# Differential attention in small blocks: the order of a software pipeline, and the place of a gelu

## The chip, the cores and the metric

The kernel runs on one core of a Trainium2 chip. A core has a matrix engine (TensorE, PE in the profile), a vector engine (VectorE, DVE), a scalar engine for activation functions (ScalarE, ACT), a general engine (GpSimd, POOL) and a queue engine (SyncE, SP). Each engine works through its own list of instructions in order and meets the others at semaphores. The metric is the device time of one execution in microseconds; lower is better.

## The reference, cut to what matters

The network is a chain of attention and feed-forward blocks on `x` of 2 x 1024 x 256, all in float32. The change is in the block that computes a differential attention with causal mask (16 heads of width 16 with two score matrices each, 4 key heads), in whose course the feed-forward block that follows it is computed too:

```python
q = _rope((x @ Wq).reshape(b, s, H, 2 * D))
k = _rope((x @ Wk).reshape(b, s, KVH, 2 * D))
v = (x @ Wv).reshape(b, s, KVH, D)
...
energy = jnp.einsum('bqhad,bkhad->bahqk', qd, kd)
energy = jnp.where(causal, NEG, energy)
scores = jax.nn.softmax(energy / np.sqrt(D), axis=-1)
diff = scores[:, 0] - lam * scores[:, 1]
diff = jnp.where(causal, NEG, diff)
diff = jax.nn.softmax(diff, axis=-1)
att = jnp.einsum('bhqv,bvhd->bqhd', diff, v)
att = att * jax.lax.rsqrt(jnp.mean(att * att, axis=-1, keepdims=True) + EPS) * rms_w
att = att * (1.0 - LAM_INIT)
return att.reshape(b, s, E) @ Wo
...
gelu = jnp.tanh(0.7978845608028654 * (gate + 0.044715 * gate ** 3)) * gate * 0.5 + gate * 0.5
out = jnp.einsum('tn,hn->th', gelu * up, Wd)
```

Here `b` is 2 and the sequence has 1024 tokens. There are two softmaxes in a row: one over the scores of each of the two matrices, and one over their difference.

## The kernel before

The stage is `attn_d_ffn1`. It goes over eight tiles `i` of 128 tokens, each for both batches. A tile has 16 pairs (two batches, eight pairs of heads each), so there are 128 pairs, and the loop at the end of the function runs one round `n` for each pair, with some more to drain. Tile `i` has `(i + 1) * 128` keys. The 64 pairs of tiles 0 to 3 (up to 512 keys) are *small*, the others *large*: these take their scores in two parts (`scores(0)`, `scores(1)`), and other PSUM pools are allocated at round 64.

A pair is an object with the steps of the work on two heads `h`, each with two score matrices `a`:

- `scores` (L1051, PE): four matmuls into two PSUM tiles `e`, of which there are two buffers, so that the next pair's scores need the maxima of this one.
- `highest` (L1062, DVE): four instructions that add the mask, write the negated scores to `p` and leave the negated row maxima in `nm`.
- `exponentials` (L1073, ACT): four activations in place, each with the row sum in `sm`.
- `ratio` (L1081, L1082 on DVE; L1086, L1090 on POOL): the reciprocals and quotients of the sums, then for each head a scaling of the second matrix and a select that masks its diagonal block.
- `difference` (L1099 on DVE; L1102, L1103 on POOL): for each head the difference of the two matrices with its row maximum, then the sign and the subtraction of the maximum.
- `turn(h)` (L1110 on PE, L1114 on ACT): the transposes of one head into the PSUM tile `dT`, of which there is one buffer, and the exponential on the way out into `pT`.
- `weigh` (L1127, PE): the product with the values, for two pairs at a time; L1136 on DVE turns the result once for eight pairs.

Every pair passes through the steps in later and later rounds: in round `n` there run the scores, maxima and exponentials of pair `n`, ratio and difference of pair `n-1`, the turns of pair `n-2` and `weigh` for pair `n-3`. The order in which they are called is the order on each engine: in this stage PE, DVE, ACT and POOL run in the order of the program (`in_order`).

Between these steps lie the *fill* steps of a round, from the table `at`: the layer norm, queries and keys of the next tile (`attn_d_inputs`, `attn_d_block`: matmuls L232, rope L259 and L268 on DVE, sums L273 and L976 on POOL, transposes L1001 and L1007, the copies L992 and L1002 on ACT), the output of the tile before (`attn_d_out`), and the feed-forward block of the tile before (`ffn1_parts`): `gate` and `up` matmuls in eight steps each (L1260; the gate's copy L1266 on ACT, the product with up L1268 on DVE), one `gelu` over the whole hidden layer (L1271, ACT) and the `down` matmuls (L1277). With `n` the first round of the tile after, gate runs in rounds `n+8` to `n+11`, gelu in `n+11`, up in `n+13` to `n+16` and down in `n+17` to `n+20`. A round's list is cut in three: a third before the first turn, a third between the turns, the rest at the end.

Of the kernel before, what the change touches and what calls it, by code (L numbers as in the profile page):

```python
# [13 lines left out]
AF = mybir.ActivationFunctionType  # L14
# [30 lines left out]
class Net:  # L45
# [772 lines left out]
    def attn_d_ffn1(self, w, wo, cos, sin, nlam, rms_w, deq):  # L818

        nc, tc = self.nc, self.tc
        NH, NKV, D = 16, 4, 16
        with ExitStack() as ctx:
            big = ctx.enter_context(tc.tile_pool(name="d_big", bufs=1))
            work = ctx.enter_context(tc.tile_pool(name="d_work", bufs=2))
            ps = ctx.enter_context(tc.tile_pool(name="d_ps", bufs=1, space=PSUM))
            self.ps = tc.alloc_tile_pool(name="d_ps0", bufs=1, space=PSUM)  # L830
            self.small = True

            nc.vector.tensor_scalar(
                wo, wo, rms_w, 1.0 - (0.8 - 0.6 * math.exp(0.0)), ALU.mult, ALU.mult
            )

            in_g = big.tile([P, 4], F32, name="in_g")
            nc.gpsimd.memset(in_g, 1.0)
            for pattern, base, cm in (([[-32, 4]], 0, 1), ([[32, 4]], 15, -1)):
                nc.gpsimd.affine_select(  # L840
                    out=in_g, in_=in_g, compare_op=ALU.is_ge, fill=0.0, base=base,
                    pattern=pattern, channel_multiplier=cm,
                )
            half = big.tile([P, 2], F32, name="half")
            nc.vector.tensor_reduce(half[:, 0:1], in_g, AX.X, ALU.add)
            nc.vector.tensor_scalar(half[:, 1:2], half[:, 0:1], -1.0, 1.0, ALU.mult, ALU.add)

            mask = big.tile([P, T], BF16, name="mask")
            nc.gpsimd.memset(mask[:, 0 : T - P], 0.0)
            nc.gpsimd.tensor_copy(mask[:, T - P : T], self.neg)  # L850
            ctx.enter_context(self.in_order())

            kT = [big.tile([P, 2, T], F32, name=f"kT{b}") for b in range(B)]
            v = [big.tile([P, NB, NKV, 32], F32, name=f"v{b}") for b in range(B)]
            for b in range(B):
                nc.gpsimd.memset(v[b][:, :, :, D:32], 1.0)
            pools = (ps, work, w, cos, sin, half, nlam, mask)
            at, pairs = {}, []  # L860

            def add(n, *steps):
                at.setdefault(max(n, -1), []).extend(steps)

            for i in range(NB):
                n = 16 * i
                tile_ = type("tile", (), {})()
                blocks = [
                    self.attn_d_block(pools, tile_, b, i, kT[b], v[b]) for b in range(B)
                ]  # L870
                for m, step in zip(
                    (-9, -8, -6, -4, -4, -2, -2, -2, -1, -1, -1, -1, -1),
                    (*self.attn_d_inputs(ps, work, tile_, i), *blocks[0][0], *blocks[1][0]),
                ):
                    add(n + m if i else -1, step)
                for _, units in blocks:
                    pairs.extend(units)

                n += 16
                squares, root, normalize, project = self.attn_d_out(ps, work, tile_, wo, i)  # L880
                if i == NB - 1:

                    for m, step in enumerate((squares, root, normalize, project)):
                        add(n + 2 + m, step)
                    continue
                stats, rows, turn, gate, gelu, up, down = self.ffn1_parts(ps, work, i, deq)
                for m, step in (
                    (2, squares), (3, root), (4, normalize), (5, project), (5, stats), (6, rows),
                    (7, turn), *((8 + k // 2, gate[k]) for k in range(8)), (11, gelu),
                    *((13 + k // 2, up[k]) for k in range(8)),  # L890
                    *((17 + k // 2, down[k]) for k in range(8)),
                ):
                    add(n + m, step)
            nothing = type("nothing", (), {"large": False})()

            def pair(n):
                return pairs[n] if 0 <= n < len(pairs) else nothing

            def do(u, name, *args):
                f = getattr(u, name, None)  # L900
                if f:
                    f(*args)

            for step in at[-1]:
                step()
            for n in range(max(at) + 1):
                if n == 16 * 4:

                    self.ps.release()
                    self.ps = tc.alloc_tile_pool(name="d_ps1", bufs=1, space=PSUM)  # L910
                    self.small = False
                fill = at.get(n, [])
                k = (len(fill) + 2) // 3, (2 * len(fill) + 2) // 3
                u, last, turned, weighed = (pair(n - j) for j in range(4))
                do(u, "scores", 0)
                do(u, "highest", 0)
                if not u.large:
                    do(u, "exponentials")
                do(weighed, "weigh")
                do(last, "ratio")  # L920
                for step in fill[: k[0]]:
                    step()
                do(turned, "turn", 0)
                if u.large:
                    u.scores(1)
                    u.highest(1)
                for step in fill[k[0] : k[1]]:
                    step()
                do(turned, "turn", 1)
                if u.large:  # L930
                    u.exponentials()
                do(last, "difference")
                for step in fill[k[1] :]:
                    step()
            self.ps.release()
# [22 lines left out]
    def attn_d_block(self, pools, tile_, b, qb, kT, v):  # L958

        nc = self.nc  # L960
# [50 lines left out]
        def pair(t, s):  # L1011

            own = type("pair", (), {})()
# [53 lines left out]
                if j == 1:  # L1067
                    nc.vector.tensor_tensor(own.nm, own.nm, nm, ALU.min)

            def exponentials():  # L1070
                for h in range(2):
                    for a in range(2):
                        nc.scalar.activation(  # L1073
                            own.p[h][a], own.p[h][a], AF.Exp,
                            bias=own.nm[:, h, a : a + 1], scale=-1.0,
                            accum_out=own.sm[:, h, a : a + 1],
                        )

            def ratio():

# [36 lines left out]
            for f in (scores, highest, exponentials, ratio, difference, turn):  # L1117
                setattr(own, f.__name__, f)
# [118 lines left out]
    def ffn1_parts(self, ps, work, i, deq):  # L1237


        nc = self.nc  # L1240
        wg, wu, wd = deq
        f = type("ffn", (), {})()
# [26 lines left out]

        def gelu():  # L1270
            nc.scalar.activation(f.inter, f.inter, AF.Gelu_apprx_tanh)  # L1271

        def down(b, quarter):
            if b == quarter == 0:
                f.po = self.bank(ps, "po").rearrange("p (b c) -> p b c", b=B)
            for m in range(4 * quarter, 4 * quarter + 4):
                nc.tensor.matmul(  # L1277
                    f.po[:, b], f.inter[:, m, b * P : (b + 1) * P],
                    wd[:, m % 2, (m // 2) * C : (m // 2 + 1) * C],
                    start=(m == 0), stop=(m == 15),  # L1280
                )
            if quarter == 3:
                xs = self.x[:, b * NB + i, :]
                nc.vector.tensor_tensor(xs, xs, f.po[:, b], ALU.add)

        return (
            stats, rows, turn, [lambda m=m: hidden(m, wg) for m in range(8)], gelu,
            [lambda m=m: hidden(m, wu) for m in range(8)],
            [lambda b=b, q=q: down(b, q) for b in range(B) for q in range(4)],
# [643 lines left out]
```

## Time and profile before

| what | value |
| --- | --- |
| time, median of 3 runs | 3122.29 us (3122.12 to 3124.22) |
| the profiled execution: time | 3129.27 us |
| its span, from first to last instruction | 3127.5 us |
| PE busy | 2628.4 us, 84% |
| DVE busy | 1923.2 us, 61% |
| ACT busy | 1351.5 us, 43% |
| POOL busy | 1031.1 us, 33% |
| mean granted clock of PE | 0.896 |

The stage of the change begins at about 1157 us (first scores, L1051) and its last scores are at 2261 us. Its groups are among the costliest of the page; each row gives line, engine, operation, output and input, count, busy time, mean duration in ns, then the idle time of the engine just before and what ended it:

```profile
L1062 DVE CUSTOM_DVE_ANT_0 p<-e,mask 128x512 f32<-128x512 f32 (+3 forms) x768 | 381.7, 553 | 106.2 <-PE e L1051 104.9
L1073 ACT ACTIVATE p<-p,nm 128x128 f32<-128x128 f32 (+7 forms) x512 | 389.9, 764 | 97.8 <-DVE nm L1062 88.2
L1086 POOL TENSOR_SCALAR p<-p,ra,neg_lam 128x128 f32<-128x128 f32 (+7 forms) x256 | 223.0, 871 | 235.3 <-DVE ra L1082 180.9
L1099 DVE CUSTOM_DVE_ANT_0 p<-p,rs 128x128 f32<-128x128 f32 (+7 forms) x256 | 207.8, 833 | 70.0 <-POOL p L1090 69.8
L1114 ACT ACTIVATE pT<-dT 128x128 f32<-128x128 f32 (+7 forms) x256 | 165.6, 647 | 285.8 <-PE dT L1110 284.5
```

The means mix blocks of 128 to 1024 keys. The column on idle time is read as: DVE stood idle for 70.0 us before the differences, nearly all of it until POOL's select at L1090 had ended.

### The profile page before, as it was taken

Reading aid. Unit: us, or ns where it says so; the run is one execution under the profiler, and the core shown is the slowest. Engines: PE = TensorE matmul, PEld = TensorE weight load, DVE = VectorE, ACT = ScalarE, POOL = GpSimd, SP = SyncE. Lnnn points to the kernel's source line nnn. Section 1 sums busy time; section 2 is a strip of 40 time slices with the busy share of each in tenths; the row PEclk is TensorE's granted clock in tenths of the full one; section 3 lists DMA queues with packets and bytes.
Section 4 is the critical chain, followed back from the end, with each engine's and each line's share of the span. In section 5 each row is a group of like instructions: output and inputs, shape, how many; then the busy total and the mean of one; then the engine's idle time right before and its main releaser. Section 6 shows DMA issues by size and latency. Waiting matters only on the chain.

```text
span 3127.5 us, 66883 instructions
## 1 busy us (share of the span) xinstructions
PE 2628.4 (84%) x26384; PEld 1618.6 (52%) x26384; DVE 1923.2 (61%) x6646; ACT 1351.5 (43%) x2712; POOL 1031.1 (33%) x1648
## 2 busy tenths in 40 slices
PE   6888889699998866887888888878878798988898
PEld 2233245343433433555555555555556577767777
DVE  4776650466765446676676777768835665665552
ACT  2785942144454335555655564655722121221110
POOL 3454210211202446565665565556620000000000
PEclk9999999699998975888899889888988899999999
DMA  3000000000000100000000000000010111001000
GB/s 112 1 1 1 1 1 0 0 1 1 1 1 26 42 15 1 1 1 1 1 1 1 1 1 1 1 1 1 1 32 16 23 23 23 14 18 36 22 10 14
DMA packets 61978, 35.38 MB, mean 11 GB/s; under 512 B 43216, under 2 KB 58080, under 8 KB 61664
## 3 DMA queue, kind: packets, MB, share of 16 engines
q1 hardware_dynamic: 59472, 29.49, 3.6%
q8 instruction: 208, 3.41, 0.4%
q10 hardware_dynamic: 2192, 1.61, 0.2%
q14 instruction: 106, 0.87, 0.1%
HBM read 22.68 MB, written 8.39 MB: 10 GB/s over the span
## 4 chain that ended last, share of the span: by engine, by line
PE 36%; DVE 13%; ACT 7%; issue 4%; POOL 3%; DMA 0%; POOLq 0%; ACTq 0%; DVEq 0%
PE ph L1260 5%; PE po L1767 4%; PE pg L1754 4%; DVE p L1062 4%; PE pu L1754 4%; PE e L1051 4%; ACT p L1073 4%; PE dT L1110 3%; POOL p L1086 2%; DVE p L1099 2%; PE po L1277 2%; PE py L1127 1%; PE pq L1437 1%; PE kh L1437 1%; PE pa L1437 1%
## 5 line engine op out<-in xcount | busy, mean ns | idle before, releaser
L1062 DVE CUSTOM_DVE_ANT_0 p<-e,mask 128x512 f32<-128x512 f32 (+3 forms) x768 | 381.7, 553 | 106.2 <-PE e L1051 104.9
L1073 ACT ACTIVATE p<-p,nm 128x128 f32<-128x128 f32 (+7 forms) x512 | 389.9, 764 | 97.8 <-DVE nm L1062 88.2
L1086 POOL TENSOR_SCALAR p<-p,ra,neg_lam 128x128 f32<-128x128 f32 (+7 forms) x256 | 223.0, 871 | 235.3 <-DVE ra L1082 180.9
L1110 PE MATMUL dT<-ident,p 128*128 128x128 f32 x1152 | 200.4, 307 | 113.0 <-ACT pT L1114 29.8
L1114 ACT ACTIVATE pT<-dT 128x128 f32<-128x128 f32 (+7 forms) x256 | 165.6, 647 | 285.8 <-PE dT L1110 284.5
L1051 PE MATMUL e<-kT,qT 32*128 32x512 f32 (+3 forms) x1536 | 234.2, 626 | 28.0 <-DVE nm L1062 26.7
L1099 DVE CUSTOM_DVE_ANT_0 p<-p,rs 128x128 f32<-128x128 f32 (+7 forms) x256 | 207.8, 833 | 70.0 <-POOL p L1090 69.8
L196 POOL TENSOR_SCALAR ln_mv<-ln_mv 128x2 f32<-128x2 f32 x48 | 15.7, 327 | 710.9 <-DVE ln_mv L194 701.0
L1110 PEld LDWEIGHTS dT<-ident,p 128*128 128x128 f32 x1152 | 154.5, 158 | 173.4 <-POOL p L1090 49.5
L723 ACT ACTIVATE pr<-s 128x512 f32<-128x512 f32 (+3 forms) x384 | 157.1, 496 | 170.2 <-PE s L718 167.0
L1103 POOL TENSOR_SCALAR p<-p,md 128x128 f32<-128x128 f32 (+7 forms) x256 | 208.3, 814 | 25.4
L437 ACT ACTIVATE pr<-s 128x1024 f32<-128x1024 f32 (+1 forms) x192 | 146.2, 823 | 122.0 <-PE s L431 119.4
L1754 PE MATMUL pg<-xT,gate 128*128 128x256 f32 x576 | 154.6, 415 | 11.0 <-issue 5.5
L1767 PE MATMUL po<-down,inter 128*128 128x256 f32 x576 | 156.8, 434 | 3.2 <-issue 2.0
L683 PE MATMUL s<-kT,qT 32*128 32x512 f32 (+3 forms) x768 | 152.4, 539 | 2.3 <-ACT pr L723 1.3
L442 ACT ACTIVATE pr<-pr 128x1024 f32<-128x1024 f32 (+1 forms) x192 | 153.1, 863 | 0.0
L691 DVE CUSTOM_DVE_ANT_0 masked<-s,mask 128x128 f32<-128x128 f32 (+3 forms) x256 | 110.7, 487 | 56.1 <-PE s L683 55.7
L1754 PE MATMUL pu<-xT,up 128*128 128x256 f32 x576 | 142.2, 391 | 0.0
L445 POOL TENSOR_SCALAR_AFFINE_SELECT pr<-pr 128x256 f32<-128x256 f32 x128 | 93.4, 746 | 143.2 <-ACT pr L442 81.9
L456 PE MATMUL py<-pr,v 128*32 128x512 f32 (+3 forms) x768 | 114.2, 531 | 27.0 <-POOL pr L445 24.9
L1767 PEld LDWEIGHTS po<-down,inter 128*128 128x128 f32 x576 | 123.5, 219 | 25.8 <-issue 2.8
L1760 DVE TENSOR_TENSOR inter<-inter,pu 128x512 f32<-128x512 f32 x72 | 49.3, 685 | 142.1 <-PE pu L1754 142.1
(302 smaller groups left out, 5446.2 us busy)
## 6 DMA issues: line engine op xcount, KB each, us to landing
uk_d<-uk SPq DMA_DIRECT2D x128, 32.0 KB, 1.9
r<-uk_d SPq DMA_DIRECT2D x8, 512.0 KB, 3.3
x<-in_L_attn_a_X SPq DMA_DIRECT2D x4, 512.0 KB, 6.1
qh_d<-qh SPq DMA_DIRECT2D x8, 256.0 KB, 2.7
o<-qh_d SPq DMA_DIRECT2D x128, 16.0 KB, 1.7
out<-x SPq DMA_DIRECT2D x4, 512.0 KB, 3.1
w<-in_L_ffn_W2T SPq DMA_DIRECT2D x1, 1024.0 KB, 8.0
pk<-in_L_ffn_gate_packed SPq DMA_DIRECT2D x8, 128.0 KB, 2.4
```

What stands on the lines that cost most here:

```text
L723: nc.scalar.activation(pr[:, g, off:512], tiles[g][:, 0:m], AF.Exp, scale=0.25)
L1051: nc.tensor.matmul(own.tiles[h][:, a, 0 : hi - lo], made["q"][r : r + 32, a, t, :], kT[r : r + 32, a, lo:hi], start=True, stop=True,)
L1062: nc.vector.tensor_tensor_reduce(own.p[h][a][:, lo:hi], own.tiles[h][:, a, 0 : hi - lo], neg_row[:, T - nk + lo : T - nk + hi], -1.0, 3e38 ...
L1073: nc.scalar.activation(own.p[h][a], own.p[h][a], AF.Exp, bias=own.nm[:, h, a : a + 1], scale=-1.0, accum_out=own.sm[:, h, a : a + 1],)
L1086: nc.gpsimd.tensor_scalar(p1, p1, own.ra[:, h : h + 1], nlam[:, head : head + 1], ALU.mult, ALU.mult)
L1099: nc.vector.tensor_tensor_reduce(p0, p0, p1, own.rs[:, h, 0:1], -3e38, ALU.add, ALU.max, md)
L1103: nc.gpsimd.tensor_scalar(p0, p0, md, 1.0, ALU.add, ALU.mult)
L1110: nc.tensor.transpose(dT[:, kb, :], own.p[h][0][:, kb * P : (kb + 1) * P], self.ident)
L1114: nc.scalar.activation(pT[:, 0 : qb + 1, :], dT[:, 0 : qb + 1, :], AF.Exp)
L1260: nc.tensor.matmul(ph[:, j, :], w[:, kc, m * P : (m + 1) * P], f.xT[:, kc, :], start=(kc == 0), stop=(kc == 1),)
L1754: nc.tensor.matmul(ph[:, j, :], m_[:, kc, m * P : (m + 1) * P], f.xT[:, kc, :], start=(kc == 0), stop=(kc == 1),)
L1767: nc.tensor.matmul(f.po[:, b], inter[m // 2][:, m % 2, b * P : (b + 1) * P], wd[:, m % 2, (m // 2) * C : (m // 2 + 1) * C], start=(m == 0) ...
```

## The change

For pairs 0 to 62 the difference moves from one to two rounds after the scores, the turns from two to three, `weigh` from three to four; the ratio stays at one. Pair 63, the last small one, keeps the old distances for difference and turns, so that it shares rounds 64 and 65 with pair 62. The large pairs keep theirs.

In a small round the order of calls is now: scores, weigh, first turn, gelu (if one is due), maxima, exponentials of the first head, two thirds of the fill, second turn, ratio, exponentials of the second head, difference, the rest of the fill. `exponentials` takes the head as its argument for this.

The gelu carries a mark `long`; such a step is taken out of the fill and run after the first turn, in the large rounds too. It is due in round `n+12` in place of `n+11`, and for tiles 0 to 2 the whole feed-forward block and the output steps come one round later than before, so that there the gelu comes in the 13th round.

```diff
                 stats, rows, turn, gate, gelu, up, down = self.ffn1_parts(ps, work, i, deq)
+                n += 1 if i < 3 else 0
...
-                    (7, turn), *((8 + k // 2, gate[k]) for k in range(8)), (11, gelu),
+                    (7, turn), *((8 + k // 2, gate[k]) for k in range(8)), (12, gelu),
...
+            first_large = 16 * 4
+            ratios, differences, turns, weighings = {}, {}, {}, {}
+            for m, u in enumerate(pairs):
+                a, b = (2, 3) if m < first_large - 1 else (1, 2)
+                for steps, lag in (
+                    (ratios, 1), (differences, a), (turns, b), (weighings, b + 1)
+                ):
+                    steps.setdefault(m + lag, []).append(u)
...
-                fill = at.get(n, [])
+                fill = [step for step in at.get(n, []) if not hasattr(step, "long")]
+                long = [step for step in at.get(n, []) if hasattr(step, "long")]
                 k = (len(fill) + 2) // 3, (2 * len(fill) + 2) // 3
-                u, last, turned, weighed = (pair(n - j) for j in range(4))
-                do(u, "scores", 0)
-                do(u, "highest", 0)
-                if not u.large:
-                    do(u, "exponentials")
-                do(weighed, "weigh")
-                do(last, "ratio")
+                u = pairs[n] if n < len(pairs) else nothing
+                if n < first_large:
+                    u.scores(0)
+                    do(weighings, n, "weigh")
+                    do(turns, n, "turn", 0)
+                    for step in long:
+                        step()
+                    u.highest(0)
+                    u.exponentials(0)
+                    for step in fill[: k[1]]:
+                        step()
+                    do(turns, n, "turn", 1)
+                    do(ratios, n, "ratio")
+                    u.exponentials(1)
+                    do(differences, n, "difference")
+                    for step in fill[k[1] :]:
+                        step()
+                    continue
+                if u.large:
+                    u.scores(0)
+                    u.highest(0)
+                do(weighings, n, "weigh")
+                do(ratios, n, "ratio")
                 for step in fill[: k[0]]:
                     step()
-                do(turned, "turn", 0)
+                do(turns, n, "turn", 0)
+                for step in long:
+                    step()
                 if u.large:
                     u.scores(1)
                     u.highest(1)
...
         def gelu():
             nc.scalar.activation(f.inter, f.inter, AF.Gelu_apprx_tanh)
+
+        gelu.long = True
```

More of the change, by code (lines that the diff above doesn't have):

```diff
@@ L894, in attn_d_ffn1, with do @@
             nothing = type("nothing", (), {"large": False})()
[L896 to L902, printed above, removed]
+            first_large = 16 * 4
[6 more added lines that the diff above has]
+                    steps.setdefault(m + lag, []).append(u)
+            def do(steps, n, name, *args):
+                for u in steps.get(n, []):
+                    f = getattr(u, name, None)
+                    if f:
+                        f(*args)
             for step in at[-1]:
                 step()
-            for n in range(max(at) + 1):
-                if n == 16 * 4:
+            for n in range(max(max(at), max(weighings)) + 1):
+                if n == first_large:
                     self.ps.release()
@@ L928, in attn_d_ffn1 @@
                     step()
-                do(turned, "turn", 1)
+                do(turns, n, "turn", 1)
                 if u.large:
-                    u.exponentials()
-                do(last, "difference")
+                    u.exponentials(0)
+                    u.exponentials(1)
+                do(differences, n, "difference")
                 for step in fill[k[1] :]:
@@ L1068, in highest, with exponentials @@
                     nc.vector.tensor_tensor(own.nm, own.nm, nm, ALU.min)
[L1070 to L1077, printed above, removed]
+            def exponentials(h):
+                for a in range(2):
+                    nc.scalar.activation(
+                        own.p[h][a], own.p[h][a], AF.Exp,
+                        bias=own.nm[:, h, a : a + 1], scale=-1.0,
+                        accum_out=own.sm[:, h, a : a + 1],
+                    )
             def ratio():
```

## The prediction

> **What bounds the kernel now.** I read the page's engine totals (no engine above PE's 84%), then the busy time by stretch, then the chain of waits and the waits inside one tile. The change lies in the differential attention stage, from about 1157 to 2290 us; its small half (blocks of up to 512 keys, rounds 0 to 63) lasts from 1160.0 to 1582.4. I cut it at the starts of the ratio (L1081): tile 0, then tiles 1, 2, 3 in two parts each, about seven rounds without and nine with gate and up matmuls. Columns: stretch, length, then busy us (instructions) of PE, weight load, DVE, ACT, POOL, granted clock, DMA share, GB/s.
>
> ```profile
> 1160.00:1230.70 70.70, 42.41 (x255) 22.97 (x254) 39.14 (x257) 37.30 (x169) 48.39 (x139) 0.58 0.00 1
> 1230.70:1269.20 38.50, 25.69 (x150) 12.92 (x151) 28.50 (x136) 19.45 (x73) 26.11 (x61) 0.50 0.00 1
> 1269.20:1332.70 63.50, 56.02 (x352) 41.67 (x351) 37.43 (x163) 38.88 (x111) 34.93 (x82) 0.94 0.01 1
> 1332.70:1380.70 48.00, 37.70 (x254) 24.21 (x253) 34.90 (x138) 24.00 (x72) 31.03 (x61) 0.79 0.00 1
> 1380.70:1449.10 68.40, 59.51 (x403) 42.94 (x402) 44.49 (x163) 44.44 (x109) 40.74 (x82) 0.95 0.00 1
> 1449.10:1506.30 57.20, 43.46 (x296) 26.77 (x295) 40.43 (x138) 28.54 (x72) 36.10 (x61) 0.76 0.00 1
> 1506.30:1582.40 76.10, 65.01 (x461) 45.98 (x459) 51.77 (x170) 47.81 (x105) 46.98 (x82) 0.96 0.01 1
> ```
>
> First parts: every engine idles a quarter or more of the time, so a loop of waits sets them. Second parts: PE is busy 85 to 88%. The chain shows the loop, here one turn of it in tile 3 from the last of four equal maxima:
>
> ```profile
> 1462.09 0.60 DVE p L1062
> 1462.83 0.17 DVE ra L1082
> 1463.17 0.77 POOL p L1086
> 1464.01 0.29 POOL p L1090
> 1464.31 1.28 POOL p L1086
> 1465.65 0.30 POOL p L1090
> 1465.98 0.75 DVE p L1099
> ```
>
> DVE takes the maxima of pair n, then the ratio of n-1, then stands until POOL has scaled n-1 (2.8 us), then takes the difference of n-1, and only then the next maxima. A second loop has the same length: ACT exponentiates n (L1073), then copies the turned block of n-2 out of PSUM (L1114, an exponential too; "copy" below), PE needs that copy for its second turn, and the next scores stand behind that turn. The waits of rounds 49 to 55 show both:
>
> ```profile
> ACT p L1073 <- DVE nm L1062: 18.6, 7, 4.8
> ...
> PE dT L1110 <- ACT pT L1114: 7.9, 4, 2.8
> ```
>
> The gelu is bracketed by two table loads; ACT is held for 6.2 us, and the next turn on PE comes 5.27 us late:
>
> ```profile
> 1289.69 1.28 ACT L1271 ACT_TABLE_LOAD   x1
> ...
> 1290.99 3.62 ACT L1271 ACTIVATE inter<-inter 128x4096 f32<-128x4096 f32 x1
> ...
> 1294.62 1.28 ACT L1073 ACT_TABLE_LOAD   x1
> ...
> 1298.40 0.66 PE L1110 MATMUL dT<-ident,p 128*128 128x128 f32 x2 [5.27 <-ACT v L992]
> ```
>
> **What the Trainium skill says.** "ScalarE: Activation LUTs", What ACT_TABLE_LOAD costs: each switch to another set of functions is a load of about 1283 ns plus a drain. The trace agrees on 1283 ns. "SBUF — State Buffer", Who interferes with whom: a DVE instruction with two SBUF inputs and a GpSimd instruction that reads SBUF exclude one another. The trace agrees: POOL's second scaling takes 1.28 us where the difference starts beside it, the first 0.77. So POOL cannot overlap the differences freely, and I price it by its means, lock included. "TensorE: Matmul & The Clock Gate", What's actually happening: an idle PE falls to half clock until it has been busy for a while. The trace has clock 0.50 to 0.79 in the first parts, 0.94 to 0.96 in the second; four transposes take 1.08 us after a gap, 0.60 otherwise.
>
> **The change, part by part.** The same instructions are issued; their order differs only in the small half and around the seven gelus.
>
> *One round more.* Difference n-2 now finds its input a round old, so DVE no longer waits for POOL. The new limit of a round without filling is the larger of two figures from mean durations. POOL, for two heads (scale + select + md + shift), tile 3: 2 x (0.90 + 0.31 + 0.25 + 0.79) = 4.5, 4.7 in the rounds measured. The loop turn, copies and exponentials, ratio, scaling, first shift, which now spans two rounds: 0.60 + 4.2 + 0.35 + 2.4 + 1.0 + 0.5 for hops (my estimate, from gaps of 0.05 to 0.2 between rows) = 9.1, or 4.6 a round. So 4.7 against 6.4 to 6.5 now. The same sum gives 2.9 against 3.5 for tile 0 (POOL 2.65, loop 5.7/2), 3.4 against 4.8 for tile 1, 4.0 against 5.4 for tile 2.
>
> Tile 0: about ten plain rounds at 0.6 = 6, and about 4 from its three long rounds (7.7, 4.4 and 10.6 us with the queries and keys), where DVE no longer meets ratio and difference in one chain: 10.
> First parts of tiles 1 to 3: the busiest engine plus a tenth for in-order losses gives 31.5 of 38.5, 40 of 48.0 and 46 of 57.2 (there PE's 43.5 is stretched by clock 0.76, so I lean on DVE's 40.4): 7 + 8 + 11 = 26.
>
> *Exponentials split around the second turn; scores, weigh and first turn ahead of the maxima.* PE gets its turned block free before ACT exponentiates, which takes away the second loop. In the second parts PE then sets the time. Its idle there is 7.5 + 8.9 + 11.1 = 27.5 us. I take 12: some 5 us a tile stays with PE waiting for queries and keys (matmul, rope on DVE, sum on POOL, transposes), and some with the gelu. The new wait: second exponentials stand on ACT behind the second copy, hence behind PE's fill. They end 0.6 + 1.6 = 2.2 us after that turn; DVE asks for them after the next scores and maxima, 1.1 + 2.5 = 3.6 us after it. Margin 1.4 us, so I price it at nothing. Queued behind that ratio on DVE are the difference and the next maxima.
>
> *Gelu.* In the small half it goes to round 13, which has no other fill, between first copy and first exponentials: still 6.2 us of ACT, with about 2 us of slack before the ratio, and PE's next first turn now waits for it. Inside the 12 above. In the large half (four gelus) it moves from the end of round 11 to behind the first copy of round 12. Near 2036 us ACT went exponentials, load, gelu, load, copy, PE's turn of 1.74, copy, exponentials: 10.0 us between the exponentials. New: first copy 0.7 wait + 0.92, 6.2, v copy 0.2, second copy 0.92 = 8.9 with the turn hidden under the gelu. 1.1 here, 0.5 near 1689, and PE's up matmuls start some us earlier; I take 1.3 x 4 = 5. From both sides: 0 and 4 x 3 = 12.
>
> *Feed-forward one round later* for tiles 0 to 2: no DMA moves, no queue of SP is passed; nothing. Hidden under 64 following rounds. *The hand-over at round 64* packs two differences and two turns into rounds 64 and 65: DVE 1.5, PE 1.2, ACT 1.2 us more there; -2.
>
> Sum: 10 + 26 + 12 + 5 - 2 = 51. In-order queues rarely reach such sums: I keep four fifths, 42. The profiled execution is 3129.27 (span 3127.5), hence 3087; the median of the runs shown lies 7 below it, so 3080 there.
>
> **Rivals.**
> A, my forecast: 3080 (gain 30 to 55).
> B, POOL and the lock become the wall: differences run beside POOL's work in every round and POOL's ops stretch to their largest (1.28, 1.34) for one more op per head: +1.1 us in the some 30 plain rounds, 33 of the 42 gone: 3113. For it: POOL is at 4.7 of the new round. Against: the differences overlap POOL's work already now.
> C, everything overlaps, PE's clock rises too: first parts at the busiest engine with PE at full clock, most of the 27.5 idle recovered, about 65: 3057. Against: queries and keys keep their serial chain.
> D, slower: the new wait of second exponentials behind PE's fill. Price: 27 rounds with gate and up; if the ratio is late by 2.0 us in each, 54 are lost and 12 of net loss remain: 3134. It decides from 42/27 = 1.6 us a round, 3.0 beyond where I put the end of the exponentials. For it: turn 1 now has two thirds of the fill ahead. Against: the margin of 1.4 and a full round of slack before the difference.
>
> **Numbers.** A 0.64, B 0.17, C 0.10, D 0.06, and 0.03 for a change that does nothing because another loop has the same length. The range runs from C's edge, 3057, to 3105, within B, to leave a fifth outside. About 0.2% is what a measurement of this kernel can tell from no change. Faster 0.91, within 0.03, slower 0.06.
>
> **What would show it.** Right: DVE's wait for POOL's select (L1090) all but gone in the small half, ratio to ratio 4.6 to 5.0 us in tile 3's plain rounds, clock in the first parts above 0.8, small half near 382 us instead of 422, large half shorter by 2 to 8. Wrong: ACT's second exponentials ending the wait of the ratio (D), POOL near 95% with its means up (B), or the second parts unchanged.

## The result and the profile after

The changed kernel takes 3168.22 us (median of 4 runs, 3156.69 to 3174.66), the kernel before 3122.36. The ratio is 1.0141, with a 95% interval of 1.0111 to 1.0172: slower by 1.4%, where the prediction had 1.3% faster. The profiled execution has a span of 3169.2 us against 3127.5, so 41.7 us more.

All of it lies in the small half: from the first maxima of pair 64 to the end it is 1555.1 us in both profiles. The first view is again the busy time by stretch, cut at the ratios of the same pairs as before (now L1111; pairs 16, 23, 32, 39, 48, 55 and 64): tile 0, then tiles 1 to 3 in two parts each. Nearly all the gate and up matmuls lie in the second parts, in both kernels. Columns: stretch, length, busy us (instructions) of PE, weight load, DVE, ACT, POOL, granted clock, DMA share, GB/s.

```profile
1160.00:1225.30 65.30, 39.28 (x252) 21.70 (x250) 37.45 (x251) 34.17 (x163) 46.65 (x134) 0.61 0.00 1
1225.30:1264.80 39.50, 23.94 (x133) 12.22 (x134) 29.14 (x144) 18.33 (x71) 25.93 (x63) 0.50 0.00 0
1264.80:1344.90 80.10, 60.46 (x369) 44.02 (x367) 36.52 (x152) 40.22 (x116) 35.14 (x82) 0.82 0.00 1
1344.90:1396.90 52.00, 35.66 (x232) 24.85 (x225) 35.84 (x145) 21.56 (x66) 30.16 (x61) 0.83 0.00 1
1396.90:1480.60 83.70, 62.31 (x424) 44.52 (x426) 44.03 (x153) 45.91 (x115) 41.28 (x82) 0.88 0.00 1
1480.60:1539.70 59.10, 40.77 (x271) 28.06 (x264) 42.79 (x146) 26.32 (x67) 34.81 (x61) 0.83 0.00 1
1539.70:1625.80 86.10, 66.76 (x476) 46.96 (x476) 51.94 (x164) 49.44 (x109) 49.64 (x86) 0.90 0.00 1
```

Lengths against before: tile 0 5.4 us shorter; the first parts 1.0, 4.0 and 1.9 longer; the second parts 16.6, 15.3 and 10.0 longer. Together 43.4, about as much as the whole. Nearly all of it is in the second parts, whose rounds have the most fill. PE's busy time over all seven stretches is the same (329.2 us, 329.8 before): what was added is waiting.

Who waits for whom, in the small half of the kernel before and then of the kernel after. A row gives engine, operand and line of the waiter, the releaser, us in total, times, longest:

```profile
DVE p L1099 <- POOL p L1090: 64.5, 74, 1.6
...
PE dT L1110 <- POOL p L1090: 26.2, 17, 2.6
...
PE dT L1110 <- ACT pT L1114: 22.6, 17, 2.8
...
PE dT L1110 <- ACT v L992: 16.0, 3, 5.4
...
PE dT L1110 <- POOL p L1103: 11.3, 9, 3.5
```

```profile
PEld dT L1140 <- POOL p L1133: 134.6, 72, 4.6
PE dT L1140 <- POOL p L1133: 92.0, 49, 4.2
...
PE dT L1140 <- ACT pT L1144: 27.6, 23, 5.8
...
DVE p L1129 <- POOL p L1120: 0.5, 3, 0.2
```

The change does remove the wait that it went for: the difference waited 64.5 us for POOL's select before, now 0.5. Its place is taken by another. PE's transposes (and the weight loads in front of them, which stand idle at the same time, so the two rows aren't added) wait for POOL's *shift*, the last of POOL's four operations on a head (L1103 before, L1133 now): 92.0 us on the matmul, 11.3 before.

The other three rows of PE before need care. The profile puts a wait for several semaphores down to the one that changed last. In all 37 waits of these rows the turn began 0.14 us after the end of an ACT copy out of `dT`, as in the row that names it, and in the rows of the shift 0.05 us after the end of a shift. So all three rows are waits for ACT's copy, 64.8 us, and the kernel after has 28.6 (27.6, and 1.0 in two more waits of this kind). The turns' waiting thus fell by 36 us for the copy and rose by 81 for the shift; the net 44 us are about what the small half grew by.

The chain of waits shows how that comes, in round 14 of tile 2. Columns: start, duration, engine with operand and line; the short "issue" pieces and some links are left out:

```profile
1442.37 0.87 PE dT L1140 x3
1443.24 5.74 PE ph L1290 x16
...
1449.01 0.69 DVE inter L1298
...
1449.82 0.17 DVE ra L1112
...
1450.16 1.26 POOL p L1116
...
1451.49 0.29 POOL p L1120
1451.79 0.65 POOL p L1116
...
1453.07 0.59 POOL p L1133
...
1453.71 0.55 PE dT L1140 x3
```

From one first turn to the next it is 11.3 us, and every link is in one round. PE turns a block and then does the fill (16 up matmuls, slow here: a gelu has just held PE up, and the granted clock in this piece is 0.61; the 16 of the next round take 3.46 us at 1.00). DVE's product with up waits for them. DVE's ratio stands behind that product, in the order of the program. POOL's scaling of pair n-1 needs the ratio, and POOL's shift of pair n-2 stands behind the scaling. PE begins the next round with the turn of exactly that pair. So the difference got a round of slack from POOL's scaling, but the turn did not get one from the shift, and the fill of PE now lies inside the loop.

### The profile page after: what moved, and what is told of

Its sections match the earlier page's. It is cut to its first block, busy times and chain, and to the rows that moved or that the text cites. A ratio compares the mean times of both kernels' runs of the same rounds, so it can differ in the third digit from the quotient of the medians.

```text
span 3169.2 us, 66946 instructions
## 1 busy us (share of the span) xinstructions
PE 2625.6 (83%) x26384; PEld 1623.9 (51%) x26384; DVE 1927.4 (61%) x6646; ACT 1346.7 (42%) x2712; POOL 1029.0 (32%) x1648
## 4 chain that ended last, share of the span: by engine, by line
PE 37%; DVE 12%; ACT 6%; POOL 5%; issue 5%; DMA 0%; POOLq 0%; ACTq 0%; DVEq 0%
PE ph L1290 5%; PE po L1799 5%; PE pg L1786 4%; PE pu L1786 4%; ACT p L1103 3%; PE dT L1140 3%; DVE p L1093 3%; PE e L1082 3%; PE po L1309 3%; POOL p L1116 2%; DVE p L1129 1%; PE py L1157 1%; PE pq L232 1%; PE pq L1469 1%; PE kh L1469 1%
## 5 line engine op out<-in xcount | busy, mean ns | idle before, releaser
L1103 ACT ACTIVATE p<-p,nm 128x128 f32<-128x128 f32 (+7 forms) x512 | 389.7, 765 | 12.4 <-DVE nm L1099 11.2
L1116 POOL TENSOR_SCALAR p<-p,ra,neg_lam 128x128 f32<-128x128 f32 (+7 forms) x256 | 229.7, 897 | 239.3 <-DVE ra L1112 156.3
L1133 POOL TENSOR_SCALAR p<-p,md 128x128 f32<-128x128 f32 (+7 forms) x256 | 205.0, 801 | 25.3
L1290 PE MATMUL ph<-xT,up 128*128 128x256 f32 x448 | 124.9, 432 | 28.0 <-DVE inter L1298 21.0
```

The costliest lines, as they stand in the source:

```text
L1103: nc.scalar.activation(own.p[h][a], own.p[h][a], AF.Exp, bias=own.nm[:, h, a : a + 1], scale=-1.0, accum_out=own.sm[:, h, a : a + 1],)
L1116: nc.gpsimd.tensor_scalar(p1, p1, own.ra[:, h : h + 1], nlam[:, head : head + 1], ALU.mult, ALU.mult)
L1133: nc.gpsimd.tensor_scalar(p0, p0, md, 1.0, ALU.add, ALU.mult)
L1290: nc.tensor.matmul(ph[:, j, :], w[:, kc, m * P : (m + 1) * P], f.xT[:, kc, :], start=(kc == 0), stop=(kc == 1),)
```

## The experiments

Two theories stood against T, the loop just described: G, that the gelu ahead of the exponentials costs the time; and S, that the second exponentials behind the fill make the ratio late, the slower rival of the prediction. A third, L, is that the added round itself costs it. Each kernel was timed against the kernel before on the same chip, whose median there was 3125 to 3130 us, against 3122 beside the kernel after. So two kernels are compared by their ratios; differences below in us are ratios times 3125.

The runs e1, e2, e8 and e11 move the same two calls of the small rounds. In the kernel after it reads as follows, with the place that each kernel gives them:

```python
u.highest(0)
u.exponentials(0)
# e1: ratio here;  e2: ratio, difference here
for step in fill[: k[1]]:
    step()
do(turns, n, "turn", 1)
do(ratios, n, "ratio")            # e11: difference first, then ratio
u.exponentials(1)
do(differences, n, "difference")
for step in fill[k[1] :]:
    step()
# e8: ratio, difference here
```

**Ratio ahead of the fill (e1).**

```diff
                     u.exponentials(0)
+                    do(ratios, n, "ratio")
                     for step in fill[: k[1]]:
                         step()
                     do(turns, n, "turn", 1)
-                    do(ratios, n, "ratio")
```

> Kernel after, with the ratio called before the fill of a small round. Theory T (late ratio): in a round with fill, DVE's ratio stands behind the fill's products and ropes, which wait for PE; POOL's scaling and the shift of the pair before stand behind it, and PE's first turn of the next round waits for that shift, so PE, DVE and POOL form one loop inside a single round. Then the ratio's part of the loop (about 2 us of POOL in some 24 rounds) goes: 3110 to 3135. Rival G (the gelu's 6.2 us ahead of the exponentials) and rival S (second exponentials behind the fill): no gain, 3160 to 3175.

Measured: 3128.52 us, ratio 1.0001 (0.9989 to 1.0013). The whole loss is gone by moving two instructions of DVE and four of POOL. It falls inside T's interval and far from the others'. It is 44 us less than the kernel after, or 1.8 a round over the 24 rounds of the expectation, which had about 2. The difference, and with it the shift, is still behind the fill here: what went out of the loop is POOL's scaling alone.

**Ratio and difference ahead of the fill (e2).**

```diff
                     u.exponentials(0)
+                    do(ratios, n, "ratio")
+                    do(differences, n, "difference")
                     for step in fill[: k[1]]:
                         step()
                     do(turns, n, "turn", 1)
-                    do(ratios, n, "ratio")
                     u.exponentials(1)
-                    do(differences, n, "difference")
```

> Kernel after, with ratio and difference both before the fill of a small round, so that nothing of POOL's work on a pair stands behind the fill. T: the whole loss goes and part of the forecast gain appears, 3085 to 3115, and PE's wait for POOL's shift (205 us on matmul and weight load in the stage's small half) falls below 60. G: no gain, 3160 to 3175. S: the ratio now asks for the second exponentials earlier, so it gets slower, above 3175.

Measured: 3117.46 us, ratio 0.9951 (0.9935 to 0.9968): faster than before, 2.5 us above T's interval. S is refuted: the ratio asks for its sums earlier, does wait 14.7 us for ACT's exponentials, and it still gets faster. T's second number failed: the wait for the shift is still long (72 us on the weight load and 42 on the matmul), because the scaling of n-1 still stands ahead of the shift of n-2 on POOL.

**The gelu back in the fill (e3).**

```diff
-                    (7, turn), *((8 + k // 2, gate[k]) for k in range(8)), (12, gelu),
+                    (7, turn), *((8 + k // 2, gate[k]) for k in range(8)), (11, gelu),
...
-        gelu.long = True
```

> Kernel after, with the gelu back in the fill, one round earlier, as the kernel before had it relative to gate and up. T: the small half stays slow, 3155 to 3175. G: most of the loss goes, 3120 to 3135. S: no gain.

Measured: 3161.6 us, ratio 1.0103 (1.0088 to 1.0119). That is some 12 us below the kernel after, whose interval (1.0111 to 1.0172) it overlaps at the edge. PE's wait for ACT's copy falls from 27.6 to 11.1 us, its wait for the shift stays at 83.2. So the gelu's place can be a part of the price, but G does not explain the loss of 44.

**Both heads' exponentials together (e4).**

```diff
                     u.exponentials(0)
+                    u.exponentials(1)
                     for step in fill[: k[1]]:
                         step()
                     do(turns, n, "turn", 1)
                     do(ratios, n, "ratio")
-                    u.exponentials(1)
```

> Kernel after, with the exponentials of both heads together ahead of the fill of a small round. T and G: within 8 us of 3168. S: most of the loss goes, 3120 to 3135.

Measured: 3183.51 us, ratio 1.0170 (1.0155 to 1.0185). That is some 9 us above the kernel after, with intervals that overlap; in the profiles, one execution each, the small half from its first maxima to those of pair 64 is 470.4 us against 456.5. S is refuted again. In us T's expectation of no change missed by 7; by the ratios it can't be told. The second copy out of the one `dT` buffer now stands behind four exponentials, but PE's wait for ACT's copies rose from 27.6 to 30.6 us only. So the split is probably worth something; how much, and by which wait, is left open.

**The round more alone, in the old order (e5).** The small rounds in the order of calls of the kernel before, with the new distances of difference, turns and `weigh`, and the gelu back in the fill; the edit is against the kernel after:

```diff
-                    (7, turn), *((8 + k // 2, gate[k]) for k in range(8)), (12, gelu),
+                    (7, turn), *((8 + k // 2, gate[k]) for k in range(8)), (11, gelu),
...
                     u.scores(0)
-                    do(weighings, n, "weigh")
-                    do(turns, n, "turn", 0)
-                    for step in long:
-                        step()
                     u.highest(0)
                     u.exponentials(0)
-                    for step in fill[: k[1]]:
+                    u.exponentials(1)
+                    do(weighings, n, "weigh")
+                    do(ratios, n, "ratio")
+                    for step in fill[: k[0]]:
+                        step()
+                    do(turns, n, "turn", 0)
+                    for step in fill[k[0] : k[1]]:
                         step()
                     do(turns, n, "turn", 1)
-                    do(ratios, n, "ratio")
-                    u.exponentials(1)
                     do(differences, n, "difference")
...
-        gelu.long = True
```

> The order of calls of the kernel before in the small rounds (maxima, all exponentials, weigh, ratio, a third of the fill, first turn, a third, second turn, difference, the rest), the gelu in the fill as there, and only the round more between difference and ratio, with the feed-forward one round later. Theory T (the loss is the ratio behind the fill, not the added round): 3090 to 3125, at or below the kernel before. Rival L (the added round itself, with the later feed-forward beside the queries and keys of the next tile, costs the time): above 3140.

Measured: 3114.59 us, ratio 0.9952 (0.9934 to 0.9970). Inside T's interval. The added round (with the feed-forward one round later) is a gain of half a per cent in the old order: L is refuted.

**The gelu moved alone (e6).** The kernel before with this, and `long` split off the fill as in the change:

```diff
-                    (7, turn), *((8 + k // 2, gate[k]) for k in range(8)), (11, gelu),
+                    (7, turn), *((8 + k // 2, gate[k]) for k in range(8)), (12, gelu),
...
                 do(turned, "turn", 0)
+                for step in long:
+                    step()
```

> The kernel before with only the gelu moved: due one round later and run after the first turn, in small and large rounds. The trace after showed the four large gelus at about nothing net (1 to 2 us won in round 11, lost again by round 14), so T expects within 8 us of the kernel before. Rival G (the gelu's place costs the time): 3140 or more.

Measured: 3113.81 us, ratio 0.9947 (0.9932 to 0.9962), better than expected, and against G. By the profiles the small half is 9.5 us shorter (405.2 against 414.7, first maxima of pair 0 to those of pair 64) of 12.5 in all, so most of the gain is made there and not in the four large gelus.

So each of the two named parts of the change wins about 0.5% by itself, and the loss comes with the new order of calls that went in with them.

**The gelu at the end of its round (e7).** From e2, in the small rounds:

```diff
                     do(turns, n, "turn", 0)
-                    for step in long:
-                        step()
                     u.highest(0)
...
                     for step in fill[k[1] :]:
                         step()
+                    for step in long:
+                        step()
```

> Ratio and difference before the fill, and in the small half the gelu at the very end of its round, behind the second exponentials. In the kernel with ratio and difference before the fill, PE stood 6.2 us for the copy behind the gelu in each of three tiles and then ran 16 up matmuls at half clock in 6.4 us instead of 3.7. If this stall is what keeps the second halves of the tiles slow, some 6 to 8 us of each of the three come back: 3093 to 3108. If not: 3110 to 3120.

The stall that it goes for reads like this in the timeline of PE in e2 (start, duration, engine, line and operation, count; in brackets the idle time before and its releaser):

```profile
1274.27 3.62 PE L1290 MATMUL ph<-xT,gate 128*128 128x256 f32 x16
...
1302.60 0.66 PE L1140 MATMUL dT<-ident,p 128*128 128x128 f32 x2 [6.20 <-ACT pT L1144]
1303.05 6.35 PE L1290 MATMUL ph<-xT,up 128*128 128x256 f32 x16
```

PE stands for 6.20 us until ACT, after gelu and two table loads, has made the copy that frees `dT`; then the up matmuls take 6.35 us where the gate's took 3.62. The granted clock is 0.57 during the former and 1.00 during the latter. Measured for e7: 3104.02 us, ratio 0.9918 (0.9899 to 0.9937), inside the interval of the expectation. That is some 10 us below e2, with intervals that just overlap; the profiles' small halves are 394.4 and 401.1 us.

**The suspected cost made larger (e8).** Ratio and difference behind all of the fill.

> The suspected cost made larger: kernel after, with ratio and difference behind all of the fill of a small round, the last third too. T: the last third's DVE and PE work (rope of the keys, one transposed block of keys, in two or three rounds a tile) joins the loop: 3172 to 3200. Rivals: no change, 3160 to 3175.

Measured: 3206.64 us, ratio 1.0241 (1.0221 to 1.0261), 6.6 us above T's interval. With e1 and e2 this is a series of doses: behind all of the fill 1.0241, behind two thirds 1.0141, ratio ahead 1.0001, both ahead 0.9951.

**Difference ahead of ratio (e9).** From e7:

```diff
                     u.exponentials(0)
-                    do(ratios, n, "ratio")
                     do(differences, n, "difference")
+                    do(ratios, n, "ratio")
```

> The kernel with ratio and difference before the fill and the gelu at the end of its round, with the difference of pair n-2 called ahead of the ratio of pair n-1. Theory T (PE's first turn waits for POOL's shift): POOL does the shift some 2 us sooner in each round, so what is left of PE's wait for it goes and the time falls to 3085 to 3100. If that wait has only become a cover for the next limit: within 5 us of 3104.

Measured: 3084.41 us, ratio 0.9865 (0.9843 to 0.9887), 0.6 us below T's interval, the fastest of all and 1.35% below the kernel before. What is left of the wait in its small half, and the second parts of tiles 2 and 3 (columns as above):

```profile
DVE p L1129 <- POOL p L1120: 14.4, 30, 1.2
PE dT L1140 <- POOL p L1133: 11.6, 18, 1.1
```

```profile
1359.50:1423.80 64.30, 57.69 (x407) 41.83 (x400) 42.71 (x161) 43.24 (x108) 39.65 (x83) 0.95 0.01 1
...
1473.60:1543.70 70.10, 64.20 (x473) 45.07 (x465) 51.98 (x170) 46.67 (x103) 47.06 (x86) 0.94 0.01 1
```

PE's longest wait for the shift is 1.1 us, where it was 4.2. The second parts of tiles 2 and 3 are down to 64.3 and 70.1 us (83.7 and 86.1 in the kernel after, 68.4 and 76.1 before), with PE busy 90 and 92%: there the busiest engine comes close to setting the time.

**Old order, round more, gelu moved (e10).** e5 with the gelu of e6:

```diff
                     do(turns, n, "turn", 0)
+                    for step in long:
+                        step()
                     for step in fill[k[0] : k[1]]:
```

> Old order of calls in the small rounds, one round more, and the gelu due one round later and run after the first turn: the two parts that each won about 15 us alone. If they add up: 3095 to 3103. If they compete for the same idle time: 3105 to 3115.

Measured: 3114.07 us, ratio 0.9961 (0.9952 to 0.9971). As in the second case of the expectation, the two gains do not add up in the time. (In the profiles the small half is 394.7 us, 20 less than before, where e5 and e6 have 16 and 9.5 less; that is one execution each.)

**One swap in the kernel after (e11).**

```diff
+                    do(differences, n, "difference")
                     do(ratios, n, "ratio")
                     u.exponentials(1)
-                    do(differences, n, "difference")
```

> Kernel after with one swap: the difference of pair n-2 ahead of the ratio of pair n-1, both still behind two thirds of the fill, the gelu where the change put it. Theory T: POOL's shift no longer stands behind its own scaling (2.0 to 2.8 us), so the loop of one round is shorter by that in some 24 rounds with fill; POOL's fill and PE's stay in it: 3105 to 3135. If the place behind the fill is all that matters: 3155 or more.

Measured: 3111.11 us, ratio 0.9959 (0.9940 to 0.9978). Inside T's interval. This swap alone turns 1.4% slower into 0.4% faster: some 57 us. Its wait for the shift, in the small half:

```profile
PE dT L1140 <- POOL p L1133: 43.0, 36, 3.7
```

That is less than half of the kernel after. The ratio is still behind the fill here, but nothing that PE waits for in the same round stands behind the ratio.

**All runs together.** The small half is from the first maxima of pair 0 to those of pair 64, and the last column is PE's wait for the shift in it, on the matmul; both are us of one profiled execution.

| kernel | ratio | small half | wait for the shift |
| --- | --- | --- | --- |
| before | 1 | 414.7 | 11.3 |
| after | 1.0141 | 456.5 | 92.0 |
| e1, ratio ahead of the fill | 1.0001 | 411.0 | 58.6 |
| e2, ratio and difference ahead | 0.9951 | 401.1 | 41.9 |
| e3, gelu back in the fill | 1.0103 | 451.4 | 83.2 |
| e4, exponentials together | 1.0170 | 470.4 | 89.7 |
| e5, old order, round more | 0.9952 | 398.5 | 10.4 |
| e6, gelu alone | 0.9947 | 405.2 | 11.7 |
| e7, e2 with the gelu at the end | 0.9918 | 394.4 | 52.1 |
| e8, both behind all the fill | 1.0241 | 485.6 | 112.8 |
| e9, e7 with difference first | 0.9865 | 370.5 | 11.6 |
| e10, e5 and e6 | 0.9961 | 394.7 | 16.6 |
| e11, difference first, behind the fill | 0.9959 | 401.3 | 43.0 |

Two things had to come together for the loss: PE's fill and POOL's scaling, one behind the other, ahead of the shift. e2 takes the fill out and leaves the scaling ahead of the shift; e11 does the reverse, and e1 takes out the scaling alone too. Each by itself removes the whole loss. e9, with neither in front of the shift (and the gelu at the end), is the fastest.

## Why the prediction was wrong

**The step that failed** is the path in *One round more*: the loop "turn, copies and exponentials, ratio, scaling, first shift, which now spans two rounds". A shorter loop was missed: ratio of n-1, scaling of n-1, shift of n-2, turn of n-2. It closes inside one round, since shift and turn belong to an older pair than ratio and scaling and are tied to them only by POOL's order. When the prediction came to the ratio behind PE's fill, it asked what stands behind it on DVE ("the difference and the next maxima"), and not on POOL, where the shift stands. PE's wait for the shift is no term of its sum; it measured 92.0 us in the small half where it had been 11.3. In tile 0, with mostly plain rounds, that left 5.4 us of gain where 10 were forecast.

**First parts.** They were priced at "the busiest engine plus a tenth for in-order losses", 26 us of gain, and became 6.9 longer.

**Second parts.** Here "PE then sets the time", and 12 us of PE's 27.5 of idle time were to be won. They became 41.9 us longer: PE's idle time in them rose to 60.4, and its busy time by 9.0 at a lower granted clock (0.82 to 0.90, 0.94 to 0.96 before). With DVE's ratio behind two thirds of the fill, PE's matmuls and DVE's products are in the same loop as POOL's scaling and shift, and a sum over three engines takes the place of the largest of them. e1, e8 and e11 change only who stands behind whom, and move the time by 44, 31 and 57 us.

**Exponentials split, first turn ahead of the maxima.** That it "takes away the second loop" was right in kind: PE's wait for ACT's copy fell from 64.8 to 28.6 us, though how much of that is the split's was not separated. The wait that was priced at nothing, second exponentials behind PE's fill, did cost nothing: in the small half after, DVE's ratio (L1111) has no wait for ACT at all. But the first turn at the head of the round is the consumer of the late shift, and of it the prediction asked only what it frees, not what it now waits for.

**Gelu.** For the small half the prediction named the wait (PE's next first turn) and then hid it in the 12 us. In e2 it is 6.2 us in the tile shown, and 2.7 more in the slow matmuls behind it; e7 against e2 puts the gelu's place at some 10 us by the ratios, 6.7 in the profiles. Of the drain that the prediction names beside the table load the trace shows nothing: in e2 the gelu starts 0.01 us after the load's end. For the large half 5 us were forecast and the trace shows nothing clear: from ratio to ratio, pair 11 of tile 6 is 1.4 us shorter and pair 14 is 1.7 us longer. Why the one follows from the other was not tested.

**The rivals.** D had the right side and the wrong place: not the exponentials are late behind the fill but the ratio itself, and not for the difference but for POOL's shift. B (POOL and the lock as the wall) did not happen, POOL is busy 44 to 71% in the stretches above. "DVE's wait for POOL's select all but gone" was right, and it was no sign of a gain.

**The size** of what overlap can win was about right. In e9, which is not the kernel of the prediction, the small half takes 379.8 us from ratio to ratio, where the prediction had 382: tile 0 wins 11.5 us, the first parts 16.2 and the second 14.8, for 10, 26 and 12 forecast. The parts were off by up to 10 us each, so that their sum, less the fifth kept back, comes so near is luck.

**Loose readings,** without weight for the result: in the first part of tile 2 PE idles some 21%, not a quarter; four fifths of 51 are 41. And a gap alone does not decide how long four transposes take: in the kernel before they took 1.08 us after 2.81 us of idle time, and 0.63 after 2.83.

## What to carry to other kernels

An extra stage of a software pipeline took away the wait of one consumer here, and left that of the next. So list, for each engine's in-order queue, what stands ahead of each producer in the new round, with the filling work, and follow every producer to the next consumer at the head of the following round: a loop that closes inside one round is a sum over engines and not a maximum. Of two steps on different pairs, put the one for the older pair first, since its consumer is nearest (e9, e11); and put filling work behind what other engines wait for (e1, e2). When a row of waits names a releaser that the waiter does not need, look for another one that ended at a fixed short time before it.

## What had not been expected

Each named part of the change wins about 0.5% alone (e5, e6), together they win 0.4% (e10), and e9 wins over three times that. The gelu's stall had a second price in the clock: 16 equal matmuls took 3.62 us and, after 6.20 us of idle time, 6.35.
